# A message-passing kernel on one core: two groups of edges through each step of the loop, with the order of VectorE and ScalarE set throughout

## The chip, the cores and the metric

One NeuronCore of one Trainium2 chip runs the whole kernel as one launch. The metric is the device time of an execution in microseconds (us), as the median of ten executions. Five engines work side by side: TensorE (PE in the profile, its weight loads PEld), VectorE (DVE), ScalarE (ACT), GpSimd (POOL) and SyncE (SP). Each takes its instructions in a fixed order; semaphores order them among each other. POOL, SP and ACT also issue DMAs.

## The reference

A layer of a graph network over 6250 nodes of 128 features and 100000 edges, sorted by destination, with 256 hidden channels:

```python
msg_in = concatenate([x[src], x[dst]], axis=-1)
h = relu(msg_in @ Wm1 + bm1)
h = relu(h @ Wm2 + bm2)
messages = h @ Wm3 + bm3
agg = segment_sum(messages, dst, 6250)
count = segment_sum(ones(100000), dst, 6250)
agg = agg / clip(count, 1)[:, None]
upd = relu(concatenate([x, agg], axis=-1) @ Wn1 + bn1) @ Wn2 + bn2
out = layernorm(x + (x + upd), axis=-1)
```

Everything is in float32.

## The kernel before

**Tables.** The first product splits into one of the source node and one of the destination node. So the kernel first makes two tables in DRAM: `atab`, 6250 rows of x times the upper half of Wm1 in float32, and `btab`, the same with the lower half, each row as three bfloat16 terms that sum to it. This stage (lines 202 to 380) runs in blocks of four tiles of 128 nodes: `turn` (L275, L279) transposes x, `a_table` (L235, L244, L245) and `b_table` (L254 to L268) multiply, copy out and store. Beside it `starts` (L290) and `columns` (L310) bring the indices into the form of the loop: `base` (L295), `tilei` (L299, the first node of each window of edges), `pbase` (L303), `srcT` (L316, the rows to gather), `dloc` (L318).

**The edge loop.** The 100000 edges are cut into 196 groups of 512 (the last has 160), a group into four windows of 128. As destinations are sorted, a window touches few nodes: at most 21 from its first one on. One group goes through these stages:
- `fetch` (L422): four indirect DMAs on the POOL queue gather 4 x 128 rows of `atab` into a slot of `ag` (L427; four slots), and four DMAs on the SP queue load each window's 22 destination rows of `btab` into `bw` (L433; four slots). The destinations themselves come in by `destinations` (L356, on the ACT queue, for two groups at a time).
- `hot` (L442): DVE compares destinations, which gives one-hot matrices `oht` (L448, destination terms) and `oh` (L451, sums).
- `first_layer` (L458): PE transposes the gathered rows into PSUM (L464, 64 rows at a time) and adds the destination terms (L470, bfloat16, 64 rows); ACT applies bias and ReLU into `h1` (L475).
- `second_layer` (L479): PE multiplies by Wm2, two halves of one PSUM bank each (L484), DVE takes the maximum with minus the bias into `h2` (L486). The rest of the bias and Wm3 are applied after the summation.
- `sums` (L488): PE multiplies `oh` with `h2`, which sums each window's edges by node (L493); ACT copies the result out as `part` (L496).
- `add_up` (L499): PE turns `part` back (L504) into PSUM tile `pt`, and DVE adds each window to its place in `acc` (L509), reading `pt` in PSUM. The places come from `tilei` by register loads (L512).

The loop (L547) is pipelined by hand. An iteration takes one group through each stage, each stage a different group: it fetches group i, and with g = i - 2 it runs add_up of g-4, first_layer of g, sums of g-3 and second_layer of g-1. After it come the last three groups, with some products of the node stage between.

**Order.** The framework plans the order of the instructions of an engine itself, save where `manual_schedule` names the engine: then it is the program's. PE's order is the program's from L220 to L619. ACT's is the program's from L222, and DVE's from L383, until iteration 6 (`turns.close()`, L549); then the framework plans both. POOL's and SP's are planned throughout.

**PSUM** has eight banks. The loop gives two to `ph` (L460), two to `ph2` (L481), one to `pg` (L491) and two to `pt` (L500).

**After the loop** a dynamic loop (L627) would handle windows with more nodes; for these inputs it runs no turn. Then the node stage (L662 on) computes the update and the norm.

Of the kernel before, what the change touches and what calls it, by code (L numbers as in the profile page):

```python
# [9 lines left out]
F32 = mybir.dt.float32  # L10
# [17 lines left out]
def kernel(  # L28
# [16 lines left out]
):  # L45

# [104 lines left out]
    with tc.tile_pool(name="prep", bufs=1) as prep, tc.tile_pool(  # L151
# [138 lines left out]
        def starts():  # L290
            for k, n in ((0, GT), (GT, GT), (RT, 2)):
                spread = pp.tile([P, GT, R], F32, name="spread", tag="pp")[:, :n]
                nc.tensor.matmul(spread, ones[:R, :], diag[:, k:k + n], start=True, stop=True)
                if k < RT:
                    nc.vector.tensor_copy(base[:, :, k:k + n], spread.rearrange("p w r -> p r w"))  # L295
                    continue
                more_w = prep.tile([1, NG], F32, name="more_w")
                nc.vector.tensor_copy(more_w.rearrange("p (r w) -> p r w", w=2), spread[0:1].rearrange("p w r -> p r w"))
            nc.vector.tensor_copy(tilei, base[0:1].rearrange("p r w -> p (r w)"))  # L299
            for h in range(2):  # L300
                half = slice(h * 2 * WN, (h + 1) * 2 * WN)
                for k in range(2):
                    nc.vector.tensor_scalar(pbase[half, :, k].rearrange("p (r s) -> p r s", s=2),  # L303
                                            base[half, :, 2 * h + k::GT], iota_p[half], None, op0=ALU.add)
# [3 lines left out]
            nc.vector.tensor_scalar(groups_i, most_more, 1.0, float(NG), op0=ALU.min, op1=ALU.mult)  # L308
# [53 lines left out]
        for i in range(BLOCKS + BEHIND):  # L362
# [47 lines left out]
    with edge, tc.tile_pool(name="wk", bufs=2) as wk, tc.tile_pool(  # L410
        name="p1", bufs=2, space=PSUM
    ) as p1, tc.tile_pool(name="p2", bufs=2, space=PSUM) as p2, tc.tile_pool(
        name="pa", bufs=1, space=PSUM
    ) as pa, tc.tile_pool(name="pt", bufs=2, space=PSUM) as ptp:


        NH2 = 4
# [4 lines left out]
        def fetch(idx, nt, firsts):  # L422


            ag = ld.tile([P, GT, H], F32, name="ag", bufs=4)
            for j in range(GT):
                nc.gpsimd.indirect_dma_start(  # L427
                    out=ag[:, j, :], out_offset=None, in_=atab[:, :],
                    in_offset=bass.IndirectOffsetOnAxis(ap=idx[:, j:j + 1], axis=0))
            bw = ld.tile([P, 2, H], BF16, name="bw", bufs=4)  # L430
            for j, first in enumerate(firsts):
                terms = btab[ds(first, WB + 1)].rearrange("n c h -> (n c) h")
                nc.sync.dma_start(bw[j // 2 * NQ:(j // 2 + 1) * NQ, j % 2, :], terms[:NQ])  # L433
            return ag, bw
# [7 lines left out]
        def hot(db, pb_cols, dl, nt):  # L442
# [3 lines left out]
            oht = wk.tile([P, 2, P], BF16, name="oht")  # L446
            for k in range(2):
                nc.vector.tensor_scalar(oht[:n, k, :], db[:n, k * P:(k + 1) * P], pb_cols[:n, k:k + 1], None,  # L448
                                        op0=ALU.is_equal)
            oh = wk.tile([P, GT, WN], F32, name="oh", bufs=4)  # L450
# [3 lines left out]
            return oht, oh  # L454
# [3 lines left out]
        def first_layer(ag, bw, oht, nt):  # L458
# [14 lines left out]
            for c in range(HC):  # L473
                for h in range(nh):
# [4 lines left out]
        def second_layer(h1, h2, nt):  # L479
            for j0 in range(0, nt, 2):  # L480
# [5 lines left out]
                nc.vector.tensor_tensor(h2[:, j0:j0 + 2, :H], ph2, nb2.to_broadcast([P, 2, H]), op=ALU.max)  # L486

        def sums(oh, h2, nt):  # L488

            n = nt * WN  # L490
            pg = pa.tile([P, H + 1], F32, name="pg")  # L491
# [7 lines left out]
        def add_up(part, firsts, nt):  # L499
            pts = [ptp.tile([P, HC + 1, NQ], F32, name="pt") for _ in range(nt // 2)]  # L500
            for c in range(HC + 1):
                for h, pt in enumerate(pts):
                    rows = part[halves[h], c * P:(c + 1) * P] if c < HC else part[halves[h], H:].to_broadcast([NQ, P])
                    nc.tensor.matmul(pt[:, c, :], rows, ident[halves[h], halves[h]], is_transpose=True,  # L504
                                     start=True, stop=True, skip_group_check=True)
            for j, first in enumerate(firsts):
                window = acc[:, :, ds(first, WB)]
                k = j % 2 * WN
                nc.vector.tensor_add(window, window, pts[j // 2][:, :, k:k + WB])  # L509
# [34 lines left out]
        ahead, lag = 2, 3  # L544
        st, hots = {}, {}
        first = list(X_FIRST)
        for i in range(NG + ahead + 1):  # L547
            if i == 6:
                turns.close()  # L549
            if i == 16:  # L550
# [6 lines left out]
            for step, after in enumerate((20, 24, 27)):  # L557
                if i >= after and (i - after) % 8 == 0 and (i - after) // 8 < len(pieces):
                    double((i - after) // 8, step)
            if i < NG:  # L560
                nt = GT if i < NGF else LT
                firsts = load_bases(tilei[0:1, i * GT:(i + 1) * GT], nt, ENG.SP)
                if i == NGF:
                    dbs = last_destinations()
                elif i % 2 == 0:
                    dbs = early.pop(0) if early else destinations(i, min(2, NGF - i), dst_row)
                st[i] = dict(nt=nt, got=fetch(srcT[:, i, :], nt, firsts), db=dbs.pop(0))
            g = i - ahead
            if 0 <= g < NG:
                s = st[g]  # L570
                ag, bw = s.pop("got")

                def make_hot(g):
                    s = st[g]
                    hots[g], s["oh"] = hot(s.pop("db"), pbase[:, g, :], dloc[:, g, :s["nt"]], s["nt"])

                if g not in hots:
                    make_hot(g)
                oht = hots.pop(g)
            k = g - lag - 1  # L580
            if 0 <= k < NG:
                s = st.pop(k)
                if "firsts" not in s:
                    s["firsts"] = load_bases(tilei[0:1, k * GT:(k + 1) * GT], s["nt"], ENG.DVE)
                add_up(s["part"], s["firsts"], s["nt"])
            if 0 <= g < NG:
                s = st[g]
                s["h1"] = first_layer(ag, bw, oht, s["nt"])
                if first:

                    make_hot(g + 1)
                    whole(x_part(first.pop(0), bank_p2, (nc.scalar, nc.vector)))
            k = g - lag
            if 0 <= k < NG:
                s = st[k]
                s["part"] = sums(s["oh"], s["h2"], s["nt"])

            m = g - 1 if g else g
            if 0 <= m < NG and "h2" not in st[m]:
                s = st[m]  # L600
                s["h2"] = h2s[m % NH2]
                second_layer(s["h1"], s["h2"], s["nt"])

        with tc.manual_schedule(engines={ENG.DVE, ENG.Activation}):
            rest = (p for b in X_END for p in x_part(b, bank_p1, (nc.scalar, nc.scalar)))
            for k in range(NG - lag, NG):
                s = st[k]
                s["firsts"] = load_bases(tilei[0:1, k * GT:(k + 1) * GT], s["nt"], ENG.DVE)
            next(rest)
            for k in range(NG - lag, NG):  # L610
                s = st[k]
                if k + 1 < NG:
                    st[k + 1]["part"] = sums(st[k + 1]["oh"], st[k + 1]["h2"], st[k + 1]["nt"])
                add_up(s["part"], s["firsts"], s["nt"])
                next(rest)
            assert next(rest, None) is None
            st.clear()
# [9 lines left out]
        with tc.For_i(0, groups, 1) as g:  # L627
# [3 lines left out]
            with tc.For_i(0, more, 1):  # L631
# [12 lines left out]
                ag, bw = fetch(idx, GT, load_bases(ti, GT, ENG.SP))  # L644
                db, = destinations(g, 1, dpad_row)
                oht, oh = hot(db, pbc, dl, GT)
                h1 = first_layer(ag, bw, oht, GT)
                second_layer(h1, h2s[0], GT)
                add_up(sums(oh, h2s[0], GT), load_bases(ti, GT, ENG.DVE), GT)
# [162 lines left out]
```

## Time and profile before

| | us |
|---|---|
| median of 10 executions | 1208.43 |
| lowest and highest | 1207.58, 1210.67 |
| the profiled execution | 1210.44 |
| its span in the trace | 1208.7 |
| tables and indices, up to the first L464 | 86.3 |
| from there to the end of the last L484 | 1039.6 |

All times of instructions below are from the start of the span. In the profile a line of the timeline has start, length, engine, line, operation, output and inputs, count, and in brackets the idle time before it with what ended it. Matmuls overlap in the pipe, so a merged line's length is from the first one's start to the last one's end. A product of float32 is issued as two instructions.

### The profile page before, as it was taken

Reading aid. Unit: us, or ns where it says so; the run is one execution under the profiler, and the core shown is the slowest. Engines: PE = TensorE matmul, PEld = TensorE weight load, DVE = VectorE, ACT = ScalarE, POOL = GpSimd, SP = SyncE. Lnnn points to the kernel's source line nnn. Section 1 sums busy time; section 2 is a strip of 40 time slices with the busy share of each in tenths; the row PEclk is TensorE's granted clock in tenths of the full one; section 3 lists DMA queues with packets and bytes.
Section 4 is the critical chain, followed back from the end, with each engine's and each line's share of the span. In section 5 each row is a group of like instructions: output and inputs, shape, how many; then the busy total and the mean of one; then the engine's idle time right before and its main releaser. Section 6 shows DMA issues by size and latency. Waiting matters only on the chain. (4 is left out here: it accounts for less than half of the span.)

```text
span 1208.7 us, 32816 instructions
## 1 busy us (share of the span) xinstructions
PE 1182.6 (98%) x11196; PEld 897.1 (74%) x11197; DVE 677.8 (56%) x2086; ACT 452.8 (37%) x1157; POOL 801.9 (66%) x862
## 2 busy tenths in 40 slices
PE   8898999999999999999999999999999999999997
PEld 6746777777777777777777777777777777777565
DVE  5864555555555555555555555555555555555587
ACT  5553333333333333333333333333333333333256
POOL 6557777777777777777777777777777777773120
PEclk9999999999999999999999999999999999999999
DMA  8786676776555555555555555555555555552243
GB/s 275 248 273 185 175 195 184 183 193 181 160 149 152 154 152 153 152 150 146 151 154 152 150 153 152 150 147 152 154 152 152 153 151 145 151 149 68 82 118 111
DMA packets 173732, 193.66 MB, mean 160 GB/s; under 512 B 30906, under 2 KB 145548, under 8 KB 173548
## 3 DMA queue, kind: packets, MB, share of 16 engines
q0 software_dynamic: 38160, 103.75, 30.8%
q1 hardware_dynamic: 106956, 61.93, 17.7%
q10 hardware_dynamic: 28448, 25.87, 8.0%
q8 instruction: 90, 1.47, 0.5%
q14 instruction: 78, 0.64, 0.2%
HBM read 168.92 MB, written 22.88 MB: 159 GB/s over the span
## 5 line engine op out<-in xcount | busy, mean ns | idle before, releaser
L427 POOL DMA_INDIRECT ag<-atab,srcT x784 | 749.3, 956 | 287.6 <-issue 181.8
L484 PE MATMUL ph<-w,h 128*128 128x256 f32 x3128 | 727.8, 386 | 0.6 <-ACT x_sb L330 0.6
L484 PEld LDWEIGHTS ph<-w,h 128*128 128x128 f32 x3128 | 578.3, 190 | 152.9 <-DVE acc L509 65.7
L475 ACT ACTIVATE h<-ph,b 128x256 f32<-128x256 f32 x782 | 307.2, 475 | 675.7 <-PE ph L470 546.4
L486 DVE TENSOR_TENSOR h<-ph,nb 128x512 f32<-128x512 f32 x391 | 270.5, 692 | 411.9 <-PE ph L484 410.8
L509 DVE TENSOR_TENSOR acc<-acc,pt 128x63 f32 x782 | 172.1, 220 | 34.6 <-PE pt L504 4.2
L464 PE MATMUL ph<-ident,ag 64*128 64x64 f32 x3128 | 130.6, 223 | 1.5 <-PE ph L328 0.9
L493 PE MATMUL pg<-h,oh 128*32 128x257 f32 x1564 | 126.0, 393 | 0.0
L464 PEld LDWEIGHTS ph<-ident,ag 64*128 64x128 f32 x3128 | 113.7, 139 | 2.6 <-issue 1.7
L448 DVE TENSOR_SCALAR oht<-db,pbase 128x128 bf16<-128x128 int32 x392 | 106.7, 357 | 1.2 <-PE ph L470 0.7
L504 PEld LDWEIGHTS pt<-ident,part 64*128 64x128 f32 x1173 | 51.0, 137 | 67.7 <-issue 64.8
L504 PE MATMUL pt<-ident,part 64*128 64x64 f32 x1173 | 77.8, 238 | 2.0 <-ACT part L496 2.0
L496 ACT COPY part<-pg 128x257 f32<-128x257 f32 x196 | 76.8, 392 | 4.0 <-PE pg L493 4.0
L470 PE MATMUL ph<-oht,bw 64*128 64x128 bf16 x1564 | 76.7, 217 | 0.9 <-DMA bw<-btab 0.6
L451 DVE TENSOR_TENSOR oh<-iota_n,dloc 128x128 f32<-128x128 f32 x196 | 54.9, 280 | 23.9 <-PE pg L493 22.0
L693 POOL TENSOR_TENSOR agg<-total,rc 128x512 f32<-128x512 f32 (+2 forms) x15 | 16.0, 1071 | 69.8 <-DVE total L690 65.9
L235 PE MATMUL pbt<-w,xT 128*128 128x256 f32 x196 | 50.4, 403 | 4.7 <-DVE groups_i L308 2.8
L470 PEld LDWEIGHTS <-bw 64*128 64x128 bf16 x1564 | 53.7, 96 | 1.6 <-DMA bw<-btab 1.4
L235 PEld LDWEIGHTS pbt<-w,xT 128*128 128x128 f32 x196 | 37.5, 201 | 13.8 <-DVE groups_i L308 3.2
L493 PEld LDWEIGHTS pg<-h,oh 128*32 128x32 f32 x1564 | 30.9, 108 | 21.8 <-issue 0.8
L264 POOL CAST bt<-rest 128x512 bf16<-128x512 f32 x18 | 11.9, 670 | 24.2 <-DVE rest L255 13.5
L716 PEld LDWEIGHTS pot<-wu,u 128*128 128x128 f32 (+1 forms) x196 | 24.0, 191 | 5.1 <-issue 4.5
(111 smaller groups left out, 422.7 us busy)
## 6 DMA issues: line engine op xcount, KB each, us to landing
bw<-btab SPq DMA_DIRECT2D x782, 32.0 KB
db<-in_dst_dram ACTq DMA_DIRECT2D x194, 128.0 KB
ag<-atab,srcT POOLq DMA_INDIRECT x784
btab<-bt SPq DMA_DIRECT2D x24, 384.0 KB
atab<-bt SPq DMA_DIRECT2D x24, 256.0 KB
xd<-in_x_dram SPq DMA_DIRECT2D x12, 256.0 KB
x2tab<-xd SPq DMA_DIRECT2D x12, 256.0 KB
x_sb<-in_x_dram SPq DMA_DIRECT2D x5, 512.0 KB
```

The source lines that it names most:

```text
L235: nc.tensor.matmul(pbt[:, a, :], xT[:, (t0 + a) * P:(t0 + a + 1) * P], w1[:, k, :], start=True, stop=True)
L427: nc.gpsimd.indirect_dma_start(out=ag[:, j, :], out_offset=None, in_=atab[:, :], in_offset=bass.IndirectOffsetOnAxis(ap=idx[:, j:j + 1], a ...
L448: nc.vector.tensor_scalar(oht[:n, k, :], db[:n, k * P:(k + 1) * P], pb_cols[:n, k:k + 1], None, op0=ALU.is_equal)
L464: nc.tensor.matmul(phs[h][:, c, u * NQ:(u + 1) * NQ], ag[halves[h], u, c * P:(c + 1) * P], ident[halves[h], halves[h]], is_transpose=True, ...
L470: nc.tensor.matmul(phs[h][:, c, k * P:(k + 1) * P], bw[halves[h], k, c * P:(c + 1) * P], oht[halves[h], k, :], start=False, stop=True, ski ...
L475: nc.scalar.activation(h1[:, c, h * 2 * P:(h + 1) * 2 * P], phs[h][:, c, :], AF.Relu, bias=b1[:, c:c + 1])
L484: nc.tensor.matmul(ph2[:, a, :], h1[:, c, (j0 + a) * P:(j0 + a + 1) * P], w2[:, c, :], start=(c == 0), stop=(c == HC - 1))
L486: nc.vector.tensor_tensor(h2[:, j0:j0 + 2, :H], ph2, nb2.to_broadcast([P, 2, H]), op=ALU.max)
L493: nc.tensor.matmul(pg[j * WN:(j + 1) * WN, :], oh[:, j, :], h2[:, j, :], start=True, stop=True, skip_group_check=True)
L496: nc.scalar.copy(part[:n, :], pg[:n, :])
L504: nc.tensor.matmul(pt[:, c, :], rows, ident[halves[h], halves[h]], is_transpose=True, start=True, stop=True, skip_group_check=True)
L509: nc.vector.tensor_add(window, window, pts[j // 2][:, :, k:k + WB])
```

## The change

- The loop takes **two groups** (a, b) through each step: add_up of both groups of step i-2, first_layer of a and of b, sums of both groups of step i-1, second_layer of a and of b. There are 98 steps; the first has its own code, as it has products of the node stage between.
- `add_up` turns both groups' part sums into two PSUM banks (one for each half of the windows), ACT copies these to `col` in SBUF, and DVE adds from `col`.
- PSUM: four banks for `ph`, two for `ph2`, two that `pg` and `pt` share. `h2` has two buffers for four, `oht` four for two.
- **Gathers**: the four gathers of group a+4 stand behind the sums. The four of b+4 stand behind a one-element copy on DVE into their slot (`gate`), which reads `h2` of a and so comes after the first half of a's second layer. In the first steps the gates read `h1` or `h2` of the groups at hand.
- **Order**: `turns.close()` stands behind the loop, so DVE's and ACT's order is the program's through all of it. `hot` is split into `terms_hot` and `edges_hot`, which stand at places of their own. The ReLUs go half by half instead of channel by channel.
- **Index copies**: `base`, `srcT` and `tilei` are copied on ACT, `pbase` is made on ACT, and `tilei` and `pbase` three to five blocks later.
- The loop for further windows calls the same functions with one group.

```diff
-                    nc.vector.tensor_copy(base[:, :, k:k + n], spread.rearrange("p w r -> p r w"))
+                    nc.scalar.copy(base[:, :, k:k + n], spread.rearrange("p w r -> p r w"))
...
+        def partition_bases(h):
+            half = slice(h * 2 * WN, (h + 1) * 2 * WN)
+            for k in range(2):
+                nc.scalar.activation(pbase[half, :, k].rearrange("p (r s) -> p r s", s=2),
+                                     base[half, :, 2 * h + k::GT], AF.Identity, bias=iota_p[half])
...
-            nc.vector.tensor_copy(
-                srcT.rearrange("p (r s) j -> p s j r", s=2)[:, s], ps)
+            nc.scalar.copy(srcT.rearrange("p (r s) j -> p s j r", s=2)[:, s], ps)
...
+            if i == INDICES + 3:
+                nc.scalar.copy(tilei, base[0:1].rearrange("p r w -> p (r w)"))
+            if i - INDICES in (4, 5):
+                partition_bases(i - INDICES - 4)
...
-            for c in range(HC):
-                for h in range(nh):
+            for h in range(nh):
+                for c in range(HC):
                     nc.scalar.activation(h1[:, c, h * 2 * P:(h + 1) * 2 * P], phs[h][:, c, :], AF.Relu,
                                          bias=b1[:, c:c + 1])
...
-        def second_layer(h1, h2, nt):
+        def second_layer(h1, h2, nt, between=None):
...
                 nc.vector.tensor_tensor(h2[:, j0:j0 + 2, :H], ph2, nb2.to_broadcast([P, 2, H]), op=ALU.max)
+                if between and not j0:
+                    between()
...
+        def add_up(parts, firsts, nts, between=None):
+            ng = len(parts)
+            pts = [pa.tile([P, ng, HC + 1, NQ], F32, name="pt", tag="pa") for _ in range(max(nts) // 2)]
+            for s, (part, nt) in enumerate(zip(parts, nts)):
+                for c in range(HC + 1):
+                    for h in range(nt // 2):
...
+                        nc.tensor.matmul(pts[h][:, s, c, :], rows, ident[halves[h], halves[h]], is_transpose=True,
+                                         start=True, stop=True, skip_group_check=True)
+            cols = []
+            for h, pt in enumerate(pts):
+                n = sum(nt // 2 > h for nt in nts)
+                col = wk.tile([P, 2, HC + 1, NQ], F32, name="col")
+                nc.scalar.copy(col[:, :n], pt[:, :n])
+                cols.append(col)
+            if between:
+                between()
...
+                    nc.vector.tensor_add(window, window, cols[j // 2][:, s, :, col:col + WB])
...
+        def fetch(g, gate=None):
+            if g % 2 == 0:
+                firsts_of[g // 2] = bases_of(g // 2, ENG.SP)
...
+            ag = rows_of_a()
+            if gate is not None:
+                nc.vector.tensor_copy(ag[0:1, 0, 0:1], gate)
+            gather(ag, srcT[:, g, :])
...
+        fetch(0)
+        fetch(1)
+        hot_terms(0)
+        for g, b in zip(pair(0), X_FIRST):
+            one_first_layer(g)
+            hot_terms(g + 1)
+            hot_edges(g)
+            whole(x_part(b, bank_p2, (nc.scalar, nc.vector)))
+            fetch(g + 2, gate=h1s[g][0:1, 0, 0:1])
+            if g == 1:
+                fetch(4)
+            one_second_layer(g)
+        fetch(5, gate=h2s[1][0:1, 0, 0:1])
+        for i in range(1, NS):
...
+            a, b = pair(i)
...
+            if i + 1 < NS:
+                hot_terms(a + 2)
+            if i >= 2:
+                ps = pair(i - 2)
+                add_up([parts.pop(g) for g in ps], bases_of(i - 2, ENG.DVE), [nts[g] for g in ps])
+            for g in (a, b):
+                one_first_layer(g)
+            for g in pair(i - 1):
+                one_sums(g)
+            if i + 2 < NS:
+                fetch(a + 4)
+
+            def between():
+                if i + 2 < NS:
+                    fetch(b + 4, gate=h2s[a % NH2][0:1, 0, 0:1])
+                if i + 1 < NS:
+                    hot_edges(a + 2)
+
+            one_second_layer(a, between)
+            if i + 1 < NS:
+                hot_terms(b + 2)
+                one_second_layer(b, lambda: hot_edges(b + 2))
+            else:
+                one_second_layer(b)
+        turns.close()
...
+            ps = pair(NS - 2)
+            add_up([parts.pop(g) for g in ps], lasts[0], [nts[g] for g in ps], between=last_sums)
             next(rest)
...
+            ps = pair(NS - 1)
+            add_up([parts.pop(g) for g in ps], lasts[1], [nts[g] for g in ps])
+            next(rest)
```

More of the change, by code (lines that the diff above doesn't have):

```diff
@@ L420, with bases, gather @@
             nc.vector.memset(t[:, :, H:], 1.0)
-        def fetch(idx, nt, firsts):
-            ag = ld.tile([P, GT, H], F32, name="ag", bufs=4)
+        def bases(firsts):
+            bw = ld.tile([P, 2, H], BF16, name="bw", bufs=4)
+            for j, first in enumerate(firsts):
+                terms = btab[ds(first, WB + 1)].rearrange("n c h -> (n c) h")
+                nc.sync.dma_start(bw[j // 2 * NQ:(j // 2 + 1) * NQ, j % 2, :], terms[:NQ])
+            return bw
+        def gather(ag, idx):
             for j in range(GT):
@@ L429, in fetch, with rows_of_a @@
                     in_offset=bass.IndirectOffsetOnAxis(ap=idx[:, j:j + 1], axis=0))
[L430 to L434, printed above, removed]
+        def rows_of_a():
+            return ld.tile([P, GT, H], F32, name="ag", bufs=4)
         def last_destinations():
@@ L497, in sums @@
             return part
[L499 to L509, printed above, removed]
+        def add_up(parts, firsts, nts, between=None):
[4 more added lines that the diff above has]
+                    for h in range(nt // 2):
+                        rows = (part[halves[h], c * P:(c + 1) * P] if c < HC
+                                else part[halves[h], H:].to_broadcast([NQ, P]))
+                        nc.tensor.matmul(pts[h][:, s, c, :], rows, ident[halves[h], halves[h]], is_transpose=True,
[8 more added lines that the diff above has]
+                between()
+            k = 0
+            for s, nt in enumerate(nts):
+                for j in range(nt):
+                    window = acc[:, :, ds(firsts[k], WB)]
+                    col = j % 2 * WN
+                    nc.vector.tensor_add(window, window, cols[j // 2][:, s, :, col:col + WB])
+                    k += 1
         def load_bases(ap, n, engine):
@@ L556 @@
                 nc.sync.dma_start(dpad[:E].rearrange("(p e) -> p e", p=16), dst.rearrange("(p e) -> p e", p=16))
[L557 to L602, printed above, removed]
+            for step, after in enumerate((10, 12, 13)):
+                if i >= after and (i - after) % 4 == 0 and (i - after) // 4 < len(pieces):
+                    double((i - after) // 4, step)
@@ new lines @@
+            a, b = pair(i)
+            if i == 1:
+                hot_terms(b)
+                hot_edges(a)
+                hot_edges(b)
+            if i + 1 < NS:
[9 more added lines that the diff above has]
+                fetch(a + 4)
@@ L605 @@
             rest = (p for b in X_END for p in x_part(b, bank_p1, (nc.scalar, nc.scalar)))
-            for k in range(NG - lag, NG):
-                s = st[k]
-                s["firsts"] = load_bases(tilei[0:1, k * GT:(k + 1) * GT], s["nt"], ENG.DVE)
-            next(rest)
[L610 to L615, printed above, removed]
+            lasts = [bases_of(i, ENG.DVE) for i in (NS - 2, NS - 1)]
```

73 lines of the change are left out of this document (48 added, 25 removed).

## The prediction

> **What bounds the kernel now.** I read the page's busy shares first, then the table of stages, then the timeline of one turn of the loop.
>
> ```profile
> PE 1182.6 (98%) x11196; PEld 897.1 (74%) x11197; DVE 677.8 (56%) x2086; ACT 452.8 (37%) x1157; POOL 801.9 (66%) x862
> ...
> 600.00:700.00 100.00, 100.00 (x1027) 77.01 (x1026) 54.07 (x172) 34.87 (x95) 72.33 (x77) 1.00 0.55 150
> ```
>
> TensorE has no idle time from 130 to 1120 us, at full clock. But a busy PE is not a PE at its peak, so the question is how its instructions follow each other. One turn, 601.29 to 606.56, takes 5.27 us, and one 500 us later, 1101.94 to 1107.21, the same.
>
> ```profile
> 600.55 0.81 PE L484 MATMUL ph<-w,h 128*128 128x256 f32 x3
> 601.29 0.40 PE L504 MATMUL pt<-ident,part 64*128 64x64 f32 x6
> 601.52 0.66 PE L464 MATMUL ph<-ident,ag 64*128 64x64 f32 x16
> 602.02 0.39 PE L470 MATMUL ph<-oht,bw 64*128 64x128 bf16 x8
> 602.34 0.64 PE L493 MATMUL pg<-h,oh 128*32 128x257 f32 x8
> 602.91 3.72 PE L484 MATMUL ph<-w,h 128*128 128x256 f32 x16
> 606.56 0.39 PE L504 MATMUL pt<-ident,part 64*128 64x64 f32 x6
> ...
> 1101.94 0.40 PE L504 MATMUL pt<-ident,part 64*128 64x64 f32 x6
> 1107.21 0.40 PE L504 MATMUL pt<-ident,part 64*128 64x64 f32 x6
> ...
> L484 PE MATMUL ph<-w,h x305: 379/379/483, 599.7 to 699.8; 128*128 128x256 f32 x153
> L464 PE MATMUL ph<-ident,ag x32: 221/222/225, 601.5 to 607.2; 64*128 64x64 f32 x32
> L470 PE MATMUL ph<-oht,bw x16: 216/216/216, 602.0 to 607.5; 64*128 64x128 bf16 x16
> ```
>
> The stages last, start to start, 0.23 (turning part sums), 0.50 (turning gathered rows), 0.32 (destination terms), 0.57 (sums) and 3.65 (second layer). Within a stage the pitch follows from the merged rows. Three L484 take 0.81 and one takes 0.379, so the pitch is (0.81 − 0.38) / 2 = 0.216; sixteen are 3.46, and 0.19 of the 3.65 lies at the stage's ends. L464 goes in pairs, eight in 0.50: 0.063 a pair. L470's four pairs have (0.39 − 0.216) / 3 = 0.058, 0.23 of 0.32: 0.09 is left. L493 goes in fours, the second about 0.24 behind the first (0.64 less its last product's 0.39): 0.48 of 0.57, 0.09 left. L504's three pairs at 0.06 are 0.18 of 0.23: 0.05 left. So **0.42 us of each turn, 8%, is spent where one stage follows another**. It looks like no wait for data: the turns are too alike for that.
>
> Next to it runs the gather queue.
>
> ```profile
> 602.46 0.95 POOL L427 DMA_INDIRECT ag<-atab,srcT  x1 [0.55 <-PE ph L470]
> 603.72 0.95 POOL L427 DMA_INDIRECT ag<-atab,srcT  x1 [0.30 <-issue]
> 604.98 0.95 POOL L427 DMA_INDIRECT ag<-atab,srcT  x1 [0.30 <-issue]
> 606.23 0.95 POOL L427 DMA_INDIRECT ag<-atab,srcT  x1 [0.30 <-issue]
> 607.73 0.95 POOL L427 DMA_INDIRECT ag<-atab,srcT  x1 [0.54 <-PE ph L470]
> ```
>
> A gather costs 1.256 us from start to start, of which 0.30 is the queue's own; four are 5.02, and 0.25 is a wait for the slot that PE has just read. POOL is thus 0.25 us a turn from being the bound.
>
> **The change part by part.** *Two groups a step.* PE does both groups' part sums, both first layers, both sums, both second layers. Each boundary is paid once for two groups, and nothing else of PE's work changes:
> - part sums: six pairs, 0.23 + 3 × 0.06 = 0.41 for 0.46;
> - first layers: 0.50 + 0.23 = 0.73 for the first, 0.82 for the second, for 1.64;
> - sums: 4 × 0.24 + 0.09 = 1.05 for 1.14;
> - second layers: 32 × 0.216 + 0.19 = 7.10 for 7.30.
>
> Sum **10.11 us a step for 10.54: 0.43 saved**. One boundary is not in the trace: destination terms of one group, then transposes of the next. Ends: nothing (the reverse, L464 to L470, adds nothing to the pitch) and 0.09 (as L470 to L493). Both are 64-row products, so I take nothing and keep 0.09 for the range.
>
> *What must hide beside it*, with t counted from the step's start. ACT gets two copies of 128x384 out of PSUM; 128x257 takes 0.39 and 128x512 0.60, so some 0.5 each.
>
> ```profile
> L496 ACT COPY part<-pg 128x257 f32<-128x257 f32 x195 | 76.4, 392 | 4.0 <-PE pg L493 4.0
> L244 ACT COPY bt<-pbt 128x512 f32<-128x512 f32 x24 | 14.0, 600 | 10.3 <-DMA atab<-bt 4.7 <-PE pbt L235 4.1 <-DMA btab<-bt 0.9
> 607.77 1.57 ACT L475 ACTIVATE h<-ph,b 128x256 f32<-128x256 f32 x4 [3.43 <-PE ph L470]
> 604.94 0.70 DVE L486 TENSOR_TENSOR h<-ph,nb 128x512 f32<-128x512 f32 x1 [1.22 <-PE ph L484]
> 602.01 1.06 DVE L509 TENSOR_TENSOR acc<-acc,pt 128x63 f32 x4
> 602.99 0.54 DVE L448 TENSOR_SCALAR oht<-db,pbase 128x128 bf16<-128x128 int32 x2
> 603.45 0.27 DVE L451 TENSOR_TENSOR oh<-iota_n,dloc 128x128 f32<-128x128 f32 x1
> ```
>
> The copies run from t = 0.65 to 1.6; their two banks are wanted again by the sums at 1.95. The first two ReLUs (0.36 apart, from their 1.57 for four) end near 2.3, and the second layer wants them at 3.0: these 0.4 and 0.7 us are the cover, and each tenth beyond it would cost 10 us in all. Behind the ReLUs on ACT stand the part copies and two index loads, needed a step later. DVE, now in fixed order, has per step 1.1 of L448, 2.1 of L509, 2.8 of L486, 0.6 of L451 and a one-element copy, 6.7 of 10.1; L509 ends at about 3.5, before the first maximum at 5.0, and each PSUM bank of the second layer has 0.7 us to spare.
>
> *Gathers in two runs.* The first run starts 0.94 after its group's transposes do (601.52 to 602.46), at t = 1.35, and keeps POOL until 6.37. The copy that releases the second stands behind the first maximum, which comes 2.03 after the second layer's start (602.91 to 604.94): 5.03, 5.72 at its end, 5.9 with the copy, 6.2 with the queue's 0.30. The gate is thus passed just before POOL gets to it. POOL needs 8 × 1.256 = 10.05, **0.06 below PE**: the next bound is already there, and less than 10.05 a step is not to be had. Queued behind the gated gather are only later gathers. SP's eight loads a step stay eight.
>
> A rule speaks against this part. The window sums L509 now read both inputs in SBUF.
>
> ```profile
> 1092.81 0.95 POOL L427 DMA_INDIRECT ag<-atab,srcT  x1 [0.30 <-PE ph L470]
> 1093.47 0.29 DVE L451 TENSOR_TENSOR oh<-iota_n,dloc 128x128 f32<-128x128 f32 x1
> ...
> L451 DVE TENSOR_TENSOR oh<-iota_n,dloc x196: 225/273/315, 86.8 to 1114.2; 128x128 f32<-128x128 f32 x195, 128x64 f32<-128x64 f32 x1
> L427 POOL DMA_INDIRECT ag<-atab,srcT x784: 947/953/1429, 72.1 to 1101.6; - x196
> ```
>
> L451 is such an instruction already. At 1093.47 it lies wholly beside a gather and takes 0.29, the gather its usual 0.95; its longest is 42 ns over its median, and half of all gathers are within 6 ns of the shortest. I take nothing for L509; the other end is a gather held for each L509's whole 0.22, priced as a rival. The Trainium skill, "SBUF — State Buffer", section "Who interferes with whom", says that a VectorE instruction with two SBUF inputs contends with a GpSimd instruction that reads SBUF, the later one blocking fully. By that rule the rival would be the result; L451's row does not bear it out.
>
> *Ramp and last step.* Before, the turn that begins at 121.72 is the seventh group's.
>
> ```profile
> 90.43 0.75 DVE L332 TENSOR_SCALAR xT<-ph,bu 128x512 f32<-128x512 f32 x1 [2.73 <-ACT h L475]
> 114.94 0.65 PE L504 MATMUL pt<-ident,part 64*128 64x64 f32 x6 [2.02 <-ACT part L496]
> 121.72 0.40 PE L504 MATMUL pt<-ident,part 64*128 64x64 f32 x6
> 125.36 0.59 SPq L531 DMA_DIRECT2D xd<-in_x_dram  x1
> 128.76 0.69 DVE L533 SCALAR_TENSOR_TENSOR xd<-xd,bu 128x512 f32<-128x512 f32 x1 [0.82 <-DMA xd<-in_x_dram]
> ```
>
> The third group's gathers now wait for DVE's L332 (done at 91.2), so the fourth group's last gather starts near 91.5 + 7 × 1.256 = 100.3, or 100.7 with its own gate; a load lands about 2.8 us after its issue (125.95 to 128.75), so PE has the rows at 103.3 and idles some 2 us. Two steps later, at 122.7, it starts groups 7 and 8 with one second layer and one sums (4.2 us) more behind it than before at 121.72: 3.2 saved. The last step saves about 0.7 by the same count of boundaries. Ends 0 and 6 together.
>
> *Index copies on ACT.*
>
> ```profile
> 36.46 3.68 DVE L299 CAST tilei<-base 1x784 int32<-1x784 f32 x1
> 41.91 0.67 DVE L255 TENSOR_TENSOR rest<-pbt,bt 128x512 f32<-128x512 f32 x1
> 42.64 1.50 PE L235 MATMUL pbt<-w,xT 128*128 128x256 f32 x4 [2.83 <-DVE groups_i L308]
> 40.00:45.00 5.00, 2.36 (x9) 2.02 (x10) 4.87 (x13) 1.01 (x2) 1.21 (x2) 0.83 0.12 41
> ```
>
> From 36.5 DVE does index work while L255 waits, and PE then stands 2.83 us. DVE loses some 7 us of it; ACT gains perhaps 4, a few per block. Ends: 5 saved (the hole is filled) and 2 lost (ACT becomes the block's bound). I take 2 saved.
>
> **Sum**: 94 steps × 0.43 = 40.4, ramp and last step 3.9, index copies 2, tail even: 46.3. 1208.7 − 46.3 = 1162.4 us of span. That execution took 1210.44 in all, 1.7 beyond its span, and 2.0 above the median of 1208.43; so the median to expect is 0.3 below the span, **1162 us**.
>
> **The rivals.**
> 1. *As summed*, 0.72. With PE's unknown boundary at 0.09 (+9), index copies at −2 (+4) and no ramp gain (+4): up to 1179. With POOL as the floor (10.05, 6 less), ramp 6 and index copies 5: down to 1151.
> 2. *Gathers a little slower, POOL the bound*, 0.08. Each 0.1 us a step that POOL loses beyond its 0.06 gives 10 us: 1172 to 1195. For it: the margin. Against it: the steady pitch of 1.256.
> 3. *The boundaries don't go*, or half of them comes back between the two first layers or as a wait for the first ReLUs: 10.33 a step, 1183. The change would then not do what it says for PE. 0.10. Against it: the boundaries sit between unlike stages only; L484 shows none inside.
> 4. *All of it comes back* in new waits, 10.54 a step: near 1205, no change, 0.03.
> 5. *The two-input sums hold the gathers*, 0.07. A gather held 0.22 for each of 8 L509 makes POOL's step 10.05 + 1.77 = 11.82, 1.28 over the present one, times 97: about **1330, slower**. It decides from 0.49 us a step (10.54 − 10.05), 28% of L509's time. Against it stands L451's row.
>
> **How the numbers follow.** Chances 0.72, 0.08, 0.10, 0.03, 0.07. Faster by over 0.2% (2.4 us, about what can be told from no change here): 1, 2 and 3, 0.90; within it 0.03; slower 0.07. The range takes in case 1 whole and most of 2 up to 1182: 1150 to 1182.
>
> **What would show it.** The timeline should have thirty-two L484 in a row, a step of 10.11 us, and one boundary of each kind in it. POOL should run almost without waits, 8 gathers in 10.05. If the second run's first gather is released by DVE, the gate binds; if L509 or the gathers lengthen, rival 5; if PE's idle column names ACT before L493 or L484, the covers of 0.4 and 0.7 were too thin. The prediction fails by more than its range if PE waits in the steady loop at all.

## The result, and the profile after

| | before | after |
|---|---|---|
| median (executions) | 1208.78 us (28) | 1156.96 us (8) |
| lowest and highest | 1207.26, 1213.35 | 1155.74, 1158.50 |
| the profiled execution, its span | 1210.44, 1208.7 | 1157.6, 1155.8 |
| tables and indices, up to the first transposes of gathered rows | 86.32 | 83.74 |
| from there to the end of the last second layer | 1039.6 | 987.8 |
| the rest of the span | 82.8 | 84.3 |

The ratio of the medians is 0.957, 95% interval 0.956 to 0.958: 52 us faster, 1157 for the 1162 forecast. Of the 52.9 us of span the loop gave 51.8 and the tables 2.6; the end lost 1.5.

The page's busy shares and one stretch of the table of stages (length, then busy time of PE, PEld, DVE, ACT and POOL with their instructions, the granted clock, DMA share, GB/s), after:

```profile
PE 1133.4 (98%) x11196; PEld 910.4 (79%) x11197; DVE 702.4 (61%) x2173; ACT 521.6 (45%) x1362; POOL 801.5 (69%) x862
```

```profile
600.00:700.00 100.00, 100.00 (x1079) 82.22 (x1078) 60.57 (x193) 43.24 (x120) 75.75 (x80) 1.00 0.60 164
```

TensorE is as full as before, with 1079 matmuls in the 100 us that held 1027. So nothing was gained by removing waits; the same products follow each other more tightly. The timeline of PE shows where, one step from its first part sum to the next:

```profile
600.38 0.58 PE L521 MATMUL pt<-ident,part 64*128 64x64 f32 x12
600.80 0.66 PE L475 MATMUL ph<-ident,ag 64*128 64x64 f32 x16
601.29 0.39 PE L481 MATMUL ph<-oht,bw 64*128 64x128 bf16 x8
601.52 0.66 PE L475 MATMUL ph<-ident,ag 64*128 64x64 f32 x16
602.02 0.39 PE L481 MATMUL ph<-oht,bw 64*128 64x128 bf16 x8
602.33 1.07 PE L506 MATMUL pg<-h,oh 128*32 128x257 f32 x16
603.34 7.17 PE L495 MATMUL ph<-w,h 128*128 128x256 f32 x32
610.44 0.58 PE L521 MATMUL pt<-ident,part 64*128 64x64 f32 x12
```

The step takes 10.06 us for the two turns of 5.27 before, and 94 of the 95 full steps take that within 0.05 us. Start to start: part sums 0.42, first layer of a 0.72, of b 0.81, sums 1.01, second layers 7.10. Terms to the next group's transposes, the boundary that the trace of before could not show, is 0.23 (601.29 to 601.52), which is the terms' own pitch: it costs nothing.

POOL beside it in the timeline; then, by source line, the gathers (all, and those from 130 to 1050 us) and the window sums (count; shortest, median and longest in ns; first and last start), and the sums of before:

```profile
603.07 0.95 POOL L436 DMA_INDIRECT ag<-atab,srcT  x1 [0.30 <-PE pg L506]
...
611.87 0.99 POOL L436 DMA_INDIRECT ag<-atab,srcT  x1 [0.30 <-DMA ag<-atab,srcT]
613.17 0.95 POOL L436 DMA_INDIRECT ag<-atab,srcT  x1 [0.30 <-PE pg L506]
```

```profile
L436 POOL DMA_INDIRECT ag<-atab,srcT x784: 949/953/1393, 69.8 to 1059.8; - x196
L436 POOL DMA_INDIRECT ag<-atab,srcT x732: 949/953/1317, 129.1 to 1049.8; - x183
L536 DVE TENSOR_TENSOR acc<-acc,col x782: 205/225/299, 108.4 to 1078.5; 128x63 f32 x196
```

```profile
L509 DVE TENSOR_TENSOR acc<-acc,pt x782: 204/221/313, 108.5 to 1131.3; 128x63 f32 x196
```

Eight gathers take 603.07 to 613.17, 10.1 us, with nothing between but the queue's own 0.30. Whatever the bracket names as the last release, no gather of this stretch waits for it. Over the loop 732 gathers start within 920.7 us (129.1 to 1049.8), one every 1.2595 us or 10.08 for eight, and no gap between them is over 0.32. So POOL, too, is without slack, a hair slower than TensorE's step; it can be, as it enters the loop ahead, and it loses some 1.5 us of that lead over the loop (an estimate: 94 steps × 0.016). Neither the gathers (953 ns, 953 before) nor the sums with two inputs in SBUF (225 for 221) have grown.

The experiments met five chips. On three of them (e1 to e4, e5, e11 and e12) the kernel before itself took 1426 to 1447 us, so of those runs only the stages ahead of the loop are compared with others.

### The profile page after: what moved, and what is told of

Its sections match the earlier page's. It is cut to its first block, busy times and chain, and to the rows that moved or that the text cites. A ratio compares the mean times of both kernels' runs of the same rounds, so it can differ in the third digit from the quotient of the medians.

```text
span 1155.8 us, 32791 instructions
## 1 busy us (share of the span) xinstructions
PE 1133.4 (98%) x11196; PEld 910.4 (79%) x11197; DVE 702.4 (61%) x2173; ACT 521.6 (45%) x1362; POOL 801.5 (69%) x862
## 5 line engine op out<-in xcount | busy, mean ns | idle before, releaser
L495 PE MATMUL ph<-w,h 128*128 128x256 f32 x3128 | 701.6, 383 | 0.8 <-DVE ag L601 0.5
L495 PEld LDWEIGHTS ph<-w,h 128*128 128x128 f32 x3128 | 587.4, 190 | 116.4 <-ACT h L486 40.7
L527 ACT COPY col<-pt 128x384 f32<-128x384 f32 x196 | 84.3, 481 | 555.6 <-PE pt L521 516.2
L486 ACT ACTIVATE h<-ph,b 128x256 f32<-128x256 f32 x782 | 297.2, 507 | 11.8 <-PE ph L475 4.7
L536 DVE TENSOR_TENSOR acc<-acc,col 128x63 f32 x782 | 177.5, 227 | 39.6 <-ACT col L527 4.6
L506 PE MATMUL pg<-h,oh 128*32 128x257 f32 x1564 | 105.3, 386 | 0.0
L455 DVE TENSOR_SCALAR oht<-db,pbase 128x128 bf16<-128x128 int32 x392 | 98.0, 310 | 2.6 <-DMA db<-in_dst_dram 2.6
L506 PEld LDWEIGHTS pg<-h,oh 128*32 128x32 f32 x1564 | 40.8, 109 | 28.0 <-ACT x_sb L330 0.8
L521 PE MATMUL pt<-ident,part 64*128 64x64 f32 x1173 | 56.7, 230 | 0.0
L766 PE MATMUL pmt<-acc,w 128*128 128x512 f32 (+2 forms) x60 | 26.2, 578 | 2.5 <-DVEq L704 2.5
```

The source lines that it names most:

```text
L486: nc.scalar.activation(h1[:, c, h * 2 * P:(h + 1) * 2 * P], phs[h][:, c, :], AF.Relu, bias=b1[:, c:c + 1])
L495: nc.tensor.matmul(ph2[:, a, :], h1[:, c, (j0 + a) * P:(j0 + a + 1) * P], w2[:, c, :], start=(c == 0), stop=(c == HC - 1))
L506: nc.tensor.matmul(pg[j * WN:(j + 1) * WN, :], oh[:, j, :], h2[:, j, :], start=True, stop=True, skip_group_check=True)
L521: nc.tensor.matmul(pts[h][:, s, c, :], rows, ident[halves[h], halves[h]], is_transpose=True, start=True, stop=True, skip_group_check=True)
L527: nc.scalar.copy(col[:, :n], pt[:, :n])
L536: nc.vector.tensor_add(window, window, cols[j // 2][:, s, :, col:col + WB])
```

## The experiments

**Is it the boundaries?** The first edit puts TensorE's stages back into the old sequence and leaves the rest of the change standing: two groups' part sums together, DVE and ACT in set order, index copies on ACT (more buffers for `h2`, `part` and `oh`, no gate).

```diff
-            for g in (a, b):
-                one_first_layer(g)
-            for g in pair(i - 1):
-                one_sums(g)
...
-            one_second_layer(a, between)
...
-                one_second_layer(b, lambda: hot_edges(b + 2))
+            one_first_layer(a)
+            if i >= 2:
+                one_sums(a - 3)
...
+            one_second_layer(a - 1, (lambda: hot_edges(a + 2)) if i + 1 < NS else None)
+            one_first_layer(b)
+            one_sums(b - 3)
...
+            one_second_layer(a, (lambda: hot_edges(b + 2)) if i + 1 < NS else None)
```

It ran three times. For the first two the kernel before was at 1428 and 1447 us, and nothing could be read of the loop (1421 and 1434 us):

> The changed kernel with TensorE's stages in the old sequence, one group after the other (first layer, sums of three groups ago, second layer of the group before), while the part sums of two groups stay together, the order of DVE and ACT stays fixed, and the index copies stay on ACT. Three buffers for h2, four for part, six for oh; the gate copy is gone. Theory A (boundaries are the gain): a step of 10.06 + 0.42 - 0.05 = 10.43 us, 95 steps, 1192 us (1187 to 1198). Rival B (fixed order and gather runs are the gain): 1157 to 1165 us.

> The kernel of e3_one_group again: there the kernel before took 1428 us and TensorE's granted clock fell in the loop, so that its time says nothing of boundaries. Where the kernel before takes about 1208 us: Theory A (boundaries are the gain): a step of 10.43 us, 1192 us (1187 to 1198). Rival B (fixed order and gather runs are the gain): 1157 to 1165 us. If the kernel before is again far above 1208 us, neither can be read.

The third run had the kernel before at 1208.5:

> The kernel of e3 and e5 a third time, on a chip where the kernel before is near 1208 us again. Theory A (boundaries are the gain): a step of 10.43 us, 1192 us (1187 to 1198). Rival B (fixed order and gather runs are the gain): 1157 to 1165 us.

Measured: 1204.7 us, ratio 0.997 (0.995 to 0.999). In the timeline of PE a step runs from 607.76 to 618.31:

```profile
607.76 0.58 PE L521 MATMUL pt<-ident,part 64*128 64x64 f32 x12
...
609.00 0.64 PE L506 MATMUL pg<-h,oh 128*32 128x257 f32 x8
609.57 3.72 PE L495 MATMUL ph<-w,h 128*128 128x256 f32 x16
613.22 0.72 PE L475 MATMUL ph<-ident,ag 64*128 64x64 f32 x16
613.77 0.39 PE L481 MATMUL ph<-oht,bw 64*128 64x128 bf16 x8
...
618.31 0.58 PE L521 MATMUL pt<-ident,part 64*128 64x64 f32 x12
```

That is 10.55 us (median 10.54), two turns of before (2 x 5.27), again without a wait. Theory A holds, rival B falls: the set order gives nothing in the steady loop (the gate is missing here; the next edit keeps it). The step was above A's 10.43, and the rows say where. The sums take 0.57 here and 1.01 for twice the products, so eight more products cost 0.44 and the boundary behind them 0.57 − 0.44 = 0.13, for the 0.09 forecast. And the transposes that follow a second layer directly take 0.55 (613.22 to 613.77) for the 0.50 elsewhere, which A left out. What happens in TensorE at such a change of stage no run shows.

The second edit moves only the sums:

```diff
-            for g in (a, b):
-                one_first_layer(g)
-            for g in pair(i - 1):
-                one_sums(g)
+            for g, k in zip((a, b), pair(i - 1)):
+                one_first_layer(g)
+                one_sums(k)
```

> The changed kernel with the sums of the two groups apart: first layer, sums, first layer, sums, then both second layers. No other work, one boundary more from terms to sums and one from sums to the next group's transposes. Theory A (TensorE is the bound and pays for each change of stage): 0.09 to 0.18 us a step more, 95 steps, 1166 to 1174 us, with no wait in PE. Rival B (the gain came from the order of DVE and ACT and from the gather runs, and boundaries are not paid twice): 1157 us, step 10.06.

> The kernel of e2 again, under the same condition. Theory A (each change of stage is paid): 0.09 to 0.18 us a step more than 10.06, 95 steps, 1166 to 1174 us, no wait in PE. Rival B (order and gather runs are the gain): 1157 us, step 10.06.

The first run (1669.9 us) can't be read. The second took 1184.2 us, ratio 0.980 (0.978 to 0.981), 27 us above the changed kernel, with a step of 10.34:

```profile
602.30 0.58 PE L521 MATMUL pt<-ident,part 64*128 64x64 f32 x12
...
603.21 0.39 PE L481 MATMUL ph<-oht,bw 64*128 64x128 bf16 x8
603.53 0.64 PE L506 MATMUL pg<-h,oh 128*32 128x257 f32 x8
604.10 0.71 PE L475 MATMUL ph<-ident,ag 64*128 64x64 f32 x16
604.65 0.39 PE L481 MATMUL ph<-oht,bw 64*128 64x128 bf16 x8
604.97 0.64 PE L506 MATMUL pg<-h,oh 128*32 128x257 f32 x8
605.54 7.17 PE L495 MATMUL ph<-w,h 128*128 128x256 f32 x32
```

Rival B falls a second time: no product was added and none waits, and yet 0.28 us a step are back. Against the changed kernel's step: the first terms 0.32 for 0.23, the second transposes 0.55 for 0.50, the two sums 0.57 each for 1.01 together; 0.09 + 0.05 + 0.13 = 0.27. A's 1166 to 1174 was too low: it priced the change from sums to the next transposes at 0.09 at most, and it took 0.13 in the sums and 0.05 in the transposes.

**Is POOL the bound?** One gather of each group is taken off POOL:

```diff
-            for j in range(GT):
+            for j in range(GT - 1):
...
+            nc.sync.dma_start(ag[:, GT - 1, :], atab[0:P, :])
```

> The changed kernel with one of the four gathers of each group taken off POOL: the rows of the fourth quarter of a group come by one plain load on SP's queue from the first 128 rows of the table, so the output's sums are not the reference's. POOL then has 6 gathers a step, 7.5 us of 10.06. Theory A (TensorE is the bound, POOL runs just below it): step 10.06, time 1157 us (1154 to 1159). Rival B (POOL, at 8 x 1.258 = 10.06 us a step, is the bound, and TensorE follows it): the step falls to what TensorE needs alone, 10.03 or less, time 1154 us and below. Where the kernel before is far above 1208 us, as with e3 and e5, only the stages before the loop can be read.

Measured: 1159.5 us, ratio 0.9575 (0.956 to 0.959), as the changed kernel's 0.957. Its timeline of PE, from one step's first part sum to the next, and that of POOL, with six gathers and a wait in each step:

```profile
599.13 0.58 PE L522 MATMUL pt<-ident,part 64*128 64x64 f32 x12
...
609.19 0.58 PE L522 MATMUL pt<-ident,part 64*128 64x64 f32 x12
```

```profile
600.48 0.95 POOL L436 DMA_INDIRECT ag<-atab,srcT  x1 [2.80 <-PE ph L482]
...
606.77 0.97 POOL L436 DMA_INDIRECT ag<-atab,srcT  x1 [0.30 <-DVE oht L456]
610.54 0.95 POOL L436 DMA_INDIRECT ag<-atab,srcT  x1 [2.79 <-PE ph L482]
```

POOL now stands 2.5 us of each step beyond its 0.30, and the step stays 10.06: TensorE needs that much by itself (theory A), and rival B falls.

The other direction adds a gather into a spare tile each step:

```diff
+            if g % 2 and g > 5:
+                spare = wk.tile([P, H], F32, name="spare", bufs=4)
+                nc.gpsimd.indirect_dma_start(
+                    out=spare, out_offset=None, in_=atab[:, :],
+                    in_offset=bass.IndirectOffsetOnAxis(ap=srcT[:, g, 0:1], axis=0))
```

> The changed kernel with one gather more a step, into a spare tile that nothing reads, from the fourth step on. Theory A (POOL has no slack left: 8 x 1.258 = 10.06 us of a step of 10.06): a step becomes 9 x 1.258 = 11.32 us, 1.26 more, 94 steps, 1275 us (1265 to 1285), and PE waits for the gathered rows. Rival B (part of the 0.30 us between gathers gives way under load): a step under 11.2, 1262 us and below.

Measured: 1272.8 us, ratio 1.053 (1.051 to 1.055). The time is A's, the way is not. Two stretches of its table of stages:

```profile
130.00:300.00 170.00, 98.45 (x845) 74.25 (x842) 45.13 (x148) 36.36 (x96) 128.37 (x136) 0.73 0.48 133
300.00:500.00 200.00, 200.00 (x2156) 164.15 (x2156) 120.02 (x383) 86.46 (x240) 151.69 (x159) 1.00 0.61 171
```

The planner put the spare gathers in bunches of four and ten between the gathers of the first steps; five steps take 27 to 29 us there, and after 300 us a step is 10.06 again. In these bunches POOL is the bound: TensorE is busy for 98.45 of the 170 us. Yet 122 gathers from 125.39 to 278.41 still follow each other every 1.265 us, so the 0.30 does not give way, and B falls. What a ninth gather does to a steady step this run does not show, as all 95 spare gathers are out by 278.41 (35 of them ahead of the step at 154.16; the 70 in the next expectation is wrong). A second version held each spare gather behind that step's second group:

```diff
+                def extra():
+                    hot_edges(b + 2)
+                    spare = wk.tile([P, H], F32, name="spare", bufs=4)
+                    nc.vector.tensor_copy(spare[0:1, 0:1], h2s[b % NH2][0:1, 0, 0:1])
+                    nc.gpsimd.indirect_dma_start(
+                        out=spare, out_offset=None, in_=atab[:, :],
+                        in_offset=bass.IndirectOffsetOnAxis(ap=srcT[:, b, 0:1], axis=0))
```

> One gather more a step as in e10, into a spare tile that nothing reads, but held by a one-element DVE copy behind the second group's first maximum, so that each step has its own: in e10 the planner put 70 of them ahead of the fourth step, and TensorE waited there. Theory A (POOL has no slack in a step): each step 9 x 1.258 = 11.32 us, PE waiting for gathered rows, 95 steps x 1.26: 1277 us (1268 to 1285). Rival B (the 0.30 us between gathers gives way under load): a step under 11.2 us, 1262 us and below.

It ran where the kernel before took 1426 us (1953.1 us), and can't be read. That POOL has no room for a ninth gather in a steady step thus rests on its pitch: 1.2595 us with no idle time in the changed kernel, 1.265 in the bunches of e10.

**Is it the set order?** `turns.close()` goes from behind the loop to the third step:

```diff
+            if i == 3:
+                turns.close()
...
-        turns.close()
```

> The changed kernel with the order of DVE and ACT left to the framework's planner from the third step on, as it was left from turn 6 on before. Theory A (TensorE is the bound, and the covers of 0.4 us for the part copies and 0.7 us for the ReLUs hold in any sensible order): 1157 us, at most 1162. Rival B (the fixed order is what makes the covers hold): some step waits for ACT appear in PE at the sums or the second layer, 0.1 us a step or more, 1167 us and above.

> The kernel of e4 again, under the same condition. Theory A (the covers of 0.4 and 0.7 us hold in any sensible order of DVE and ACT): 1157 us, at most 1162. Rival B (the fixed order is what makes them hold): PE waits for ACT or DVE at the sums or the second layer, 0.1 us a step or more, 1167 us and above.

The first run (2014.5 us) can't be read. The second: 1170.7 us, ratio 0.968 (0.966 to 0.970), 14 us above the changed kernel. The time is B's, the way is not. PE has no waits in the steady loop, and its step is 10.06; the loss is in three steps of 19.9, 11.7 and 14.4 us. DVE's timeline at the first:

```profile
108.12 1.35 DVE L536 TENSOR_TENSOR acc<-acc,col 128x63 f32 x5
118.91 0.69 DVE L561 SCALAR_TENSOR_TENSOR xd<-xd,bu 128x512 f32<-128x512 f32 x1 [9.44 <-DMA xd<-in_x_dram]
119.52 0.74 DVE L536 TENSOR_TENSOR acc<-acc,col 128x63 f32 x3
```

The planner drew the doubling of x (L561) ahead of its load, which then held 9.44 us of sums and maxima behind it; L561 waits 3.60 and 4.73 us again in the two other steps. So the covers of 0.4 and 0.7 us don't hang on the order (A), but the order guards against one operation that waits for a late load at the head of DVE's queue.

**The index copies.** Back on DVE, in their old places:

```diff
-                    nc.scalar.copy(base[:, :, k:k + n], spread.rearrange("p w r -> p r w"))
+                    nc.vector.tensor_copy(base[:, :, k:k + n], spread.rearrange("p w r -> p r w"))
...
+            nc.vector.tensor_copy(tilei, base[0:1].rearrange("p r w -> p (r w)"))
+            for h in range(2):
+                partition_bases(h)
...
-            nc.scalar.copy(srcT.rearrange("p (r s) j -> p s j r", s=2)[:, s], ps)
+            nc.vector.tensor_copy(srcT.rearrange("p (r s) j -> p s j r", s=2)[:, s], ps)
```

> The changed kernel with the index copies back on DVE, where they stood (base, tilei, pbase, srcT); all else as changed. Theory A (the index copies are worth what the start of the edge stage shows: the first transposes of gathered rows began at 83.74 for 86.32): the start goes back by 2.6 us, time 1159.5 us (1158.5 to 1161). Rival B (DVE is held by POOL's memsets there in any case, and the earlier start comes from another edit): start near 83.7, time 1157.

Of its 1967.8 us only the tables can be read. PE's timeline, the hole and the last product of that stage:

```profile
42.14 2.08 PE L236 MATMUL pbt<-w,xT 128*128 128x256 f32 x4 [2.83 <-DVE groups_i L306]
85.91 0.50 PE L399 MATMUL pb<-b,w 128*128 128x1 f32 x4
```

The hole of 2.83 us is back. The last product starts at 85.9, and at 81.0, 81.3 and 82.0 in e2, e3 and e4, on the same chip with the copies on ACT: they are worth 4 to 5 us there. The changed kernel's profile has it at 82.6, the latest of the eleven kernels that have these copies and the casts below in place (81.0 to 82.6), so A's 2.6 is the low end; rival B falls.

One more part of that stage was open. In the changed kernel DVE and POOL ran:

```profile
34.80 4.90 POOL L395 MEMSET acc<- 128x784 f32 x7
...
36.29 3.52 DVE L300 CAST morei<-more_w 1x196 int32<-1x196 f32 x1
```

and before, POOL beside the 3.68 us of `tilei`'s cast:

```profile
34.12 5.59 POOL L391 MEMSET acc<- 128x784 f32 x8
```

A cast of 196 elements takes as long as one of 784, and both end within 0.5 us of the end of the memsets (39.70, 39.71). In e1, where the larger cast goes first again, the smaller one follows behind the memsets and takes 0.25:

```profile
35.97 3.68 DVE L300 CAST tilei<-base 1x784 int32<-1x784 f32 x1
40.98 0.25 DVE L303 CAST morei<-more_w 1x196 int32<-1x196 f32 x1
```

So that cast, with the two small operations behind it, went last:

```diff
-            nc.vector.tensor_copy(morei, more_w)
...
+        counts(more_w)
         pb3 = pp.tile([P, 1], F32, name="pb3", tag="pp")
```

> The changed kernel with the three small DVE operations that count further windows (cast of morei, reduction, groups_i) moved behind the table loop; all else as changed. In the changed kernel the cast of 196 elements took 3.52 us, from 36.29 to 39.81, while POOL zeroed acc from 34.80 to 39.70; before, a cast of 784 elements ended at the end of the same burst of memsets. Theory A (the cast is held by POOL's memsets, not by its own size): without it DVE starts the next subtraction of rest at about 36.3 for 40.17, the hole of 0.87 us in PE near 41 goes, the edge stage starts 1 to 2 us earlier: 1155 to 1156 us; moved, the cast takes 0.3 us. Rival B (the cast is slow by itself): it takes 3.5 us in its new place too. Rival C (the tables wait for something else): edge stage starts at 83.7 as before, 1157 us.

The tables can be read (the whole, 1963.9 us, can't). The cast's group, and DVE and PE in the timeline:

```profile
L303 DVE CAST morei<-more_w x1: 240/240/240, 80.9 to 80.9; 1x196 int32<-1x196 f32 x1
```

```profile
34.81 0.34 DVE L299 COPY more_w<-spread 1x196 f32<-1x196 f32 x1
35.08 0.69 DVE L256 TENSOR_TENSOR rest<-pbt,bt 128x512 f32<-128x512 f32 x1
...
80.00 0.50 PE L404 MATMUL pb<-b,w 128*128 128x1 f32 x4
```

Theory A holds: 0.24 us in its new place, DVE goes on at once, and the last product starts at 80.00, 1.5 us ahead of e12's 81.53 on the same chip and 1.0 ahead of the earliest of the eleven. B and C fall; the size is known to about 1 us, by which e2 and e4 differ on one chip. The Trainium skill, "SBUF — State Buffer", section "Who interferes with whom", says that a VectorE cast in a two-port mode and a GpSimd instruction exclude each other for a whole instruction. The trace agrees as to the wait, and shows it longer: over five memsets in a row, not one. That this cast ran in such a mode no row shows. The changed kernel with this edit should thus gain 1.5 us (an estimate from those two rows); it was not timed where the two kernels could be compared.

## Why the prediction was right, point by point

- **What bounds the kernel**: right. PE was and is without idle time, and of the 0.84 us of boundaries in two turns a step saves 0.48. e7, which gives back the boundaries alone, gives back all that a step had gained.
- **Step of 10.11**: 10.06. Part sums, first layers and second layers came as summed (0.42, 0.72 and 0.81, 7.10). The mis-sized term is the sums, 1.01 for 1.05: the pitch was read as 0.24 from one merged row, and is 0.22, as for the second layer. Over 94 steps that is 4.7 us. The unknown boundary was nothing, the end taken.
- **What must hide beside it**: right. Part copies, ReLUs and maxima hold no matmul in the steady loop, in the program's order or in the planner's (e9).
- **Gathers in two runs**: right that POOL would be the next bound and the gate be passed just in time; POOL's margin is nothing, where 0.06 was forecast. What the gate holds was wrong. It writes a single element of the slot's first quarter, so only that one of four gathers waits for DVE, and the planner is free to put it last.
- **Ramp and last step, 3.9**: some 7. The step that failed is "the third group's gathers now wait for DVE's L332". POOL's timeline:

```profile
84.59 1.09 POOL L436 DMA_INDIRECT ag<-atab,srcT  x1 [0.30 <-issue]
88.59 0.95 POOL L436 DMA_INDIRECT ag<-atab,srcT  x1 [2.91 <-DVE ag L601]
```

Twelve gathers, from 69.80 to 84.59, were out ahead of the first gate: groups one and two, and four more of the next two. The fourth group's transposes began at 97.86 right behind the third's, with no wait of 2 us; two steps later PE was at 116.9 (106.85 + 10.06), not 122.7. That makes the ramp 121.72 − 116.92 and the 4.2 more behind it, less the tables' 2.6: 6.4. The last step gave under 1.
- **Index copies, 2**: 2.6 in this profile, 4 to 5 by e1. "DVE loses some 7 us" overlooked that the cast's 3.68 was a wait for POOL, which the next cast took over (3.52 for its 0.24).
- **Tail even**: it lost 1.5.
- The misses add up: 4.7 + 3.2 + 0.6 − 1.5, and −0.6 for one step of 10.65 in which PE waited 0.38 for a late gather, are 6.4 of the 6.6 us by which the span's gain beat the forecast.
- **Rivals**: 2, 3 and 4 fell by the step. Rival 5 fell by the rows of gathers and sums. The Trainium skill, "SBUF — State Buffer", section "Who interferes with whom", whose rule spoke for it, says further down that such a DVE instruction takes only the read side of the shared ports while descriptor generation needs the write side, and marks this as inferred. The trace agrees with that sentence (225 ns for 221, 953 for 953).

## What to carry to other kernels

A TensorE that shows 100% can still have several per cent to give: add up the pitch inside each stage and compare it with start-to-start times; what is over is paid at each change of stage, and falls when stages of one kind are put together. Before going further look at the neighbour: here POOL's eight gathers take 10.08 us beside TensorE's 10.06, so by that pitch the next boundary saved would be worth next to nothing until a gather is. And read a long instruction's end beside the other engines' ends before pricing it by size.

## What was not expected of the hardware

On three chips every kernel was slower, and those that put two groups together most: the kernel before 1426 to 1447 us at a mean granted clock of 0.99, one group at a time (e3, e5) 1421 and 1434, two groups 1670 at 0.95 with the sums apart (e2), and 1953 to 2014 at 0.86 to 0.87 otherwise (e1, e4, e11, e12). Two groups, 4% faster on the other chips, were 37% slower there (e11, which differs from the changed kernel by three small operations: ratio 1.375, 1.370 to 1.381). In PE's timeline there are gaps that the profile puts down to nothing it shows ("issue"), among the destination terms with one group (e5, first) and within the second layers with two (e11):

```profile
903.22 0.66 PE L475 MATMUL ph<-ident,ag 64*128 64x64 f32 x16
903.72 0.36 PE L481 MATMUL ph<-oht,bw 64*128 64x128 bf16 x2
904.57 0.36 PE L481 MATMUL ph<-oht,bw 64*128 64x128 bf16 x6 [0.49 <-issue]
```

```profile
914.02 1.07 PE L510 MATMUL pg<-h,oh 128*32 128x257 f32 x16
915.02 0.48 PE L499 MATMUL ph<-w,h 128*128 128x256 f32 x1
915.69 0.38 PE L499 MATMUL ph<-w,h 128*128 128x256 f32 x1 [0.18 <-issue]
...
917.85 4.96 PE L499 MATMUL ph<-w,h 128*128 128x256 f32 x13 [0.97 <-issue]
```

A step of e5 takes 12.7 us for e7's 10.54 with the same instructions, about 1 us more a group; e11's second layers take 15.3 us (915.02 to 930.27) for 7.1. What makes these chips do so was not found, and the changed kernel itself was not run there.
